# A two-layer graph network: the second layer's first product made of seven products of quarters, x read twice, the column factors stored with the adjacency

## The chip, the cores and the metric

The kernel runs on one core of a Trainium2 chip. The time is device microseconds of that core. TensorE (PE) multiplies; VectorE (DVE), ScalarE (ACT) and GpSimd (POOL) do the elementwise work; SyncE (SP) issues most loads, and POOL issues the stores. Each engine works through its own list of instructions in order and waits on semaphores for the others. All data is float32.

## What is computed

The input is x, 16 graphs of 1024 nodes with 256 channels, and one adjacency matrix of 1024 by 1024.

```
# layer 0
h = max(layernorm(x), 0)
c = mean of h over channels
A_s = weights made of sigmoid(c[m] - c[n]);  g = relu((h.T @ (adj * A_s)) * para)
q = g.T;  k, v = h @ kv_w;  4 heads of 64
x = x + softmax(q k.T * scale) v
# layer 1
h = max(layernorm(x), 0)
A_hat = (adj + I) * dinv[:, None] * dinv[None, :]       # dinv from row and column sums
agg = A_hat @ h
y1 = agg @ W1.T + b1                                    # 256 -> 512 channels
y2 = relu(batchnorm(y1)) @ W2.T + b2                    # statistics over all graphs
x = x + batchnorm(y2)
```

## The kernel before

**Stages.** A short beginning handles graph 0's first norm, keys and queries. Then `attention` (L1092) goes through 16 graphs of 16 steps. A step computes scores of two blocks of 128 keys (`scores`, L923, PE L933, exponentials on ACT L941), adds up the exponentials on DVE (`Unit.add`, L962 and L965) and multiplies the exponentials of the step before with the values (`Unit.values`, PE L976). Between these, each step takes pieces from a generator, `background(b)` (L835), which holds everything else that must happen while graph b's attention runs. A `total` of costs (1.71 for two products of 128x128 by 512) is spread over the 16 steps: each step takes pieces until its share is done. After the last graph, `second` (L1221) does the second batch-normalised product and the output.

**What the background of graph b holds, in this order.** Keys and values of graph b+1 (`keys_values`, L649), its queries (`queries`, L514: the product with the weighted adjacency, as seven products of quarters), the second norm of graph b-1 (`normed`, L790), the aggregation of graph b-1 (`aggregate`, L682: again seven products of quarters, with the combined quarters of A_hat read from `aht_d` in DRAM), the first norm of graph b+2 (`summed`) and, in `prepare` (L812), the first product of layer 1 for graph b-1 (`hidden`, L757) woven with the first weights of graph b+2 (`weigh`, L454: ACT L485 and L493, then DVE L472).

**`hidden` before.** For each half of the nodes and each of four blocks of 128 output channels, two products of 128x128 by 512 are accumulated in one PSUM bank, evicted with the bias by ACT (L773), stored by a POOL DMA (L774), and read by DVE for the batch statistics (L777): 16 products and 8 evictions for a graph. All background products take turns in three PSUM banks (`ps_mm`, `bank`, L164), so a product waits until the one three before it has been evicted.

**The graph's matrix.** In graph 0's background, `degrees` (L225) sums rows and columns and forms dinv; `graph` (L244) reads the adjacency in 8 pieces, adds the identity, forms the seven combined quarters with four subtractions on POOL (L278, L279, L282, L283) and stores them to `aht_d` (L285 to L287). The two run side by side with graph 1's queries. The row factor dinv[n] goes into the second norm's scale (`shift`, L325, DVE L328). The column factor is applied to the aggregate after the products: `scale` (L705) multiplies the four quarters of `at` with `dbc`, dinv broadcast to all partitions, which `load_later` (L290) fetches through DRAM (`dinv_d`).

**x.** `load_x` (L173) loads a graph's x once into a pool of three buffers; it serves the first norm, receives the attention's output (`add_output`, L1058) and then feeds the second norm. `keep` (L786) stores it to DRAM.

Of the kernel before, what the change touches and what calls it, by code (L numbers as in the profile page):

```python
# [10 lines left out]
F32 = mybir.dt.float32  # L11
# [6 lines left out]
P = 128  # L18
# [5 lines left out]
def gnn_two_layers_kernel(  # L24
# [72 lines left out]
    def layers(shifted):  # L97
# [20 lines left out]
        ps_mm = st.enter_context(tc.tile_pool(name=f"ps_mm_{kind}", bufs=3, space=PSUM))  # L118

        xs, hs, hts, ats, qs, ks, vs = {}, {}, {}, {}, {}, {}, {}  # L120
        invs = {}
        csums, cbcs, weighted, weighers = {}, {}, {}, {}
        s1s = {}
# [48 lines left out]

        def load_x(b):  # L173
            xs[b] = p3.tile([P, NT, C], F32, tag="x", name=f"x_{b}")
            parts = 4 if b == 0 else 2
            for part in range(parts):
                t = slice(part * NT // parts, (part + 1) * NT // parts)
                nc.sync.dma_start(
                    out=xs[b][:, t], in_=x[b].rearrange("(t p) c -> p t c", p=P)[:, t]
                )  # L180
# [44 lines left out]
        def degrees():  # L225

            nc.vector.tensor_reduce(row, rows.rearrange("p q t -> p t q"), AX.X, ALU.add)
            ahead = [load_adj_t(t, "at") for t in range(2)]
            yield 0.0
            for t in range(NT):  # L230
                a = ahead[t]
                blk = a[:, t * P : (t + 1) * P]
                nc.scalar.activation(a, a, AF.Copy, accum_out=col[:, t : t + 1])
                db = p1.tile([P, P], F32, tag="s1", name=f"db_{t}")
                nc.vector.tensor_mul(db, blk, ident)
                nc.vector.tensor_reduce(diag[:, t : t + 1], db, AX.X, ALU.add)
# [4 lines left out]
            nc.vector.tensor_sub(deg, deg, diag)  # L241
            rsqrt(dinv, deg, 1.0, tmp_deg)

        def graph():  # L244
# [21 lines left out]
            for u in range(2 * HT):  # L266
# [21 lines left out]
                yield 0.0  # L288

        def load_later():  # L290
            later["w1"] = big.tile([P, CC, H1], F32, tag="w1", name="w1")
            nc.sync.dma_start(out=later["w1"], in_=w1_t.rearrange("(k p) j -> p k j", p=P))
            later["dbc"] = const.tile([P, N], F32, tag="dbc", name=f"dbc_{kind}")
            nc.sync.dma_start(out=dinv_d.rearrange("(t p) -> p t", p=P), in_=dinv)
            nc.sync.dma_start(
                out=later["dbc"], in_=dinv_d.rearrange("(o n) -> o n", o=1).to_broadcast([P, N])
            )

        class Norm:
# [3 lines left out]
            def __init__(self, b, first):  # L303
                tag = "a" if first else "b"
                self.src = xs[b]
                self.st6 = p1.tile([P, NT, 6], F32, tag="st6", name=f"st6_{tag}_{b}")
# [375 lines left out]
        def aggregate(b):  # L682


            pieces = []
            order = (0, 2, 5, 1, 4, 6, 3)

# [24 lines left out]
            def second(m):  # L712
                add(c11, m, c12)
                sub(a12, a12, a11)
                soon(lambda: scale(c11, 0))

            def fifth(m):
                add(c22, m, c21)
                add(c12, m, c12)
                soon(lambda: scale(c22, 1))  # L720

            def sixth(m):
                add(c21, m, c21)
                soon(lambda: scale(c21, 0))

            def seventh(m):
                add(c12, m, c12)
                scale(c12, 1)

            for i, (left, after) in enumerate(  # L730
# [12 lines left out]
                for th in range(NP // 2):  # L743
# [68 lines left out]
        def prepare(b, products):  # L812
# [3 lines left out]
            yield from islice(products, 1)  # L816
            if b == 2:
                for k in range(CC):
                    yield from weave(islice(products, 3), (0, islice(w, AHEAD // 2)))
                    yield TOP  # L820
                    transposed(b, (k,))
                    yield 1.0
                yield from products
                return
            squares(b)
            yield from weave(islice(products, 3), (0, islice(w, AHEAD // 2)))
            gathered(b, 0)
            yield from weave(islice(products, 1), (0, islice(w, 1)))
            gathered(b, 1)
            yield from weave(islice(products, 2), (0, islice(w, AHEAD // 2 - 1)))  # L830
            yield from products
# [3 lines left out]
        def background(b):  # L835

            if b == 0:
                differences(1)
                for k in range(CC):
# [15 lines left out]
            gather = aggregate(b - 1)  # L855
            if b + 1 < B:
                w, products, norm = weighers[b + 1], keys_values(b + 1), normed(b - 1)
                yield from weave(islice(products, 4), (0, islice(w, 4)))
                if b == 1:
                    load_later()  # L860
                yield from weave(queries(b + 1), (0, double(w)), (9, islice(norm, 5)))
                yield next(gather)
                yield from weave(products, (0, norm))
            else:
                yield from weave(endings.pop(), (2, normed(b - 1)))
                yield next(gather)
            if b + 2 < B:
# [224 lines left out]
        def attention():  # L1092
# [7 lines left out]
            for s in range(len(steps) + 2):  # L1100
                if s < len(steps):
                    unit, g = steps[s]
                    b = unit.at[0]
                    if s % per_graph == 0:
# [25 lines left out]
                if before is not None:  # L1130
                    (last, g_last), prs = before
                    last.values(g_last, prs)
                    if g_last == NG - 1:
# [29 lines left out]
        with st:  # L1163
# [22 lines left out]
            else:  # L1186
# [23 lines left out]
                run(weave(products, (0, islice(weighers[0], AHEAD))))  # L1210
                load_x(1)
                load_x(2)
                run(weave(plain_queries(0), (0, weighers[0]), (5, Norm(1, True).all())))
                attention()
                attn.close()
# [348 lines left out]
```

## Time and profile before

| what | value |
|---|---|
| median of 3 runs | 2489.24 us (2488.99 to 2489.55) |
| the profiled execution | 2488.76 us |
| its span, first to last instruction | 2487.0 us |
| mean granted TensorE clock | 0.993 |
| PE busy, share of the span | 2435.7 us, 98% |
| DVE, ACT, POOL busy | 1882.0, 1401.7, 429.2 us |
| moved by DMA | 421.42 MB, 169 GB/s on average |

A group in the profile names a line, an engine, an operation, the tiles out<-in, how often it occurred, the busy time, the mean duration of one in ns, and the idle time of the engine just before, with what ended it. In the timeline the columns are the start and the duration in us. A float32 product appears as two matmul records for each half of 64 columns, four for a product of 128x128 by 512. In a table of stretches, each engine's busy time is given with the number of its instructions in brackets.

### The profile page before, as it was taken

To read this page: it belongs to the slowest core of one execution; us is meant where nothing else is said; L and a number is where in the kernel's file an instruction comes from. 1 tells how busy PE (TensorE), PEld (TensorE's weight loads), DVE (VectorE), ACT (ScalarE), POOL (GpSimd) and SP (SyncE) were. 2 spreads that over 40 slices of the span, in tenths; PEclk is the share of its full clock that TensorE was granted. 3 is DMA by queue.
4 is the path that set the end of the run, shared out by engine and by line. 5 is a ranking of instruction groups with operands and counts; after the bars stand their busy time and mean duration, and the time that the engine had idled before them with its cause. 6 is when DMAs were issued, how large, how long until landed. Compare 5 with 4: busy or idle time off the path is not lost. (4 is left out here: it accounts for less than half of the span.)

```text
span 2487.0 us, 35569 instructions
## 1 busy us (share of the span) xinstructions
PE 2435.7 (98%) x13403; PEld 841.2 (34%) x13403; DVE 1882.0 (76%) x2920; ACT 1401.7 (56%) x1927; POOL 429.2 (17%) x527
## 2 busy tenths in 40 slices
PE   9999999999999999999999999999999999999995
PEld 4333333333333333333333333333333332334444
DVE  5668787877778787878787787868787877767775
ACT  7775564647473746656474747465564634345544
POOL 1640101010101001011101010110101001036652
PEclk9999999999999999999999999999999999999997
DMA  4754535354545545362645445543536344355559
GB/s 150 238 173 172 170 114 199 101 199 129 197 145 178 164 159 169 116 206 84 215 126 182 145 174 169 178 153 132 191 94 210 116 140 162 132 214 220 189 199 374
DMA packets 187909, 421.42 MB, mean 169 GB/s; under 512 B 21832, under 2 KB 81744, under 8 KB 181968
## 3 DMA queue, kind: packets, MB, share of 16 engines
q1 hardware_dynamic: 158560, 311.56, 37.9%
q0 software_dynamic: 29168, 107.50, 11.6%
q8 instruction: 108, 1.77, 0.3%
q14 instruction: 73, 0.60, 0.1%
HBM read 315.63 MB, written 103.35 MB: 168 GB/s over the span
## 5 line engine op out<-in xcount | busy, mean ns | idle before, releaser
L941 ACT ACTIVATE p<-sc 128x1024 f32<-128x1024 f32 x512 | 494.9, 1019 | 617.6 <-PE sc L933 617.2
L965 DVE TENSOR_TENSOR acc<-acc,p 128x1024 f32<-128x1024 f32 x384 | 471.3, 1227 | 165.1 <-ACT p L941 143.8
L933 PE MATMUL sc<-q,k 64*64 64x512 f32 x4096 | 498.8, 602 | 6.2 <-ACT p L941 6.2
L976 PE MATMUL o<-p,v 128*64 128x512 f32 x2048 | 494.5, 604 | 0.3 <-DVE os L990 0.3
L171 PE MATMUL pg<-w,h_a 128*64 128x512 f32 x1600 | 359.8, 592 | 0.8 <-DVE w L472 0.8
L171 PE MATMUL pa<-aht,h_b 128*64 128x512 f32 x1536 | 346.0, 592 | 1.1 <-ACT h_b L342 1.0
L485 ACT ACTIVATE w<-cbc,csum 128x512 f32<-128x512 f32 x256 | 285.8, 1168 | 0.0
L933 PEld LDWEIGHTS sc<-q,k 64*64 64x64 f32 x4096 | 131.0, 132 | 347.9 <-issue 286.5
L472 DVE SCALAR_TENSOR_TENSOR w<-w,adj 128x1024 f32<-128x1024 f32 x128 | 156.9, 1225 | 95.0 <-ACT w L493 91.1
L171 PE MATMUL py<-at,w 128*64 128x512 f32 x1024 | 228.4, 592 | 0.2 <-ACT y L773 0.2
L976 PEld LDWEIGHTS o<-p,v 128*64 128x64 f32 x2048 | 124.4, 136 | 298.3 <-issue 260.3
L994 POOL DMA_DIRECT2D out_d<-os x58 | 34.2, 590 | 1070.8 <-DVE os L990 1037.5
L171 PEld LDWEIGHTS pg<-w,h_a 128*64 128x64 f32 x1600 | 114.8, 137 | 229.2 <-issue 218.8
L171 PEld LDWEIGHTS pa<-aht,h_b 128*64 128x64 f32 x1536 | 109.9, 137 | 215.3 <-issue 202.0
L773 ACT ACTIVATE y<-py,vec 128x512 f32<-128x512 f32 x128 | 87.4, 683 | 115.4 <-PE py L171 91.8
L493 ACT ACTIVATE w<-w 128x1024 f32<-128x1024 f32 x128 | 135.1, 1055 | 1.7
L774 POOL DMA_DIRECT2D y_d<-y x128 | 69.7, 545 | 371.8 <-ACT y L773 362.6
L548 DVE TENSOR_TENSOR w<-w,w 128x1024 f32<-128x1024 f32 x112 | 132.7, 1214 | 1.5
L171 PEld LDWEIGHTS py<-at,w 128*64 128x64 f32 x1024 | 74.0, 137 | 145.5 <-issue 131.5
L171 PE MATMUL pv<-kvw_f,ht 128*64 128x256 f32 x1024 | 116.1, 379 | 0.0
L171 PE MATMUL pk<-ht,kvw_f 128*64 128x512 f32 x512 | 115.2, 592 | 0.2 <-ACT ht L404 0.2
L342 ACT ACTIVATE h_b<-x,lnsm_b 128x256 f32<-128x256 f32 x128 | 69.9, 599 | 65.9 <-DVE lnsm_b L331 65.9
(169 smaller groups left out, 2665.4 us busy)
## 6 DMA issues: line engine op xcount, KB each, us to landing
aht<-aht_d SPq DMA_DIRECT2D x224, 512.0 KB, 6.4
adj<-in_adj_dram SPq DMA_DIRECT2D x128, 512.0 KB, 4.8
y_d<-y POOLq DMA_DIRECT2D x128, 256.0 KB, 3.0
yin_f<-y_d SPq DMA_DIRECT2D x32, 1024.0 KB, 6.4
para<-in_para_dram SPq DMA_DIRECT2D x64, 256.0 KB, 3.6
x_d<-x POOLq DMA_DIRECT2D x16, 1024.0 KB, 5.2
xo_f<-x_d SPq DMA_DIRECT2D x32, 512.0 KB, 8.2
out_dram<-xo_f POOLq DMA_DIRECT2D x32, 512.0 KB, 10.8
```

The source lines that it names most:

```text
L171: nc.tensor.matmul(dst[r], left[:, r], right, start=start, stop=stop)
L342: nc.scalar.activation(self.h[:, t, :], self.src[:, t, :], AF.Relu, bias=self.sm[:, 1, t : t + 1], scale=self.sm[:, 0, t : t + 1], accum_o ...
L472: nc.vector.scalar_tensor_tensor(w, w, 1.0, a, op0=ALU.add, op1=ALU.mult)
L485: nc.scalar.activation(w[:, t, :].rearrange("p (t q) -> p t q", q=P), cbc[:, q * NT // NH : (q + 1) * NT // NH], AF.Abs, bias=csum[:, th * ...
L493: nc.scalar.activation(made[i], made[i], AF.Tanh, scale=-0.5 / C)
L548: nc.vector.tensor_sub(block(i)[part], block(x)[part], block(y)[part])
L773: nc.scalar.activation(y, made, AF.Identity, bias=b1[:, j : j + 1])
L774: nc.gpsimd.dma_start(out=y1_d[i][:, j, :], in_=y)
L933: nc.tensor.matmul(sc[part, e, :], ks[b][k][r, m * P + c * HW : m * P + (c + 1) * HW], qs[b][k][r, f * FB : (f + 1) * FB], start=True, sto ...
L941: nc.scalar.activation(pr, sc, AF.Exp)
L965: nc.vector.tensor_add(self.acc, self.acc, pr)
L976: nc.tensor.matmul(self.o[r, :], vs[b][k][:, m, r], pr[:, e, :], start=(m == 0), stop=(m == NT - 1),)
```

## The change

In `hidden`, graphs 0 to 13 now compute the first product of layer 1 from quarters of W1 and of the aggregate: seven products for each of two blocks of 128 columns, 14 in all, none accumulated with another. Four combinations of W1's quarters are formed once on POOL (`load_later`); four combinations of the aggregate's quarters are formed on DVE for each graph (`steps_of` and the first line of `hidden`). Two of the seven products are evicted by ACT, five by DVE, which adds the parts that belong together; POOL adds two further pairs for each block. Graphs 14 and 15 keep the old form (`plain_hidden`).

The column factor moves from `aggregate` into `graph`: each piece of the adjacency is multiplied by `dbc` on POOL (two multiplications a piece) before it is combined, so `graph` now has to follow `degrees` and the fetching of `dbc`, and runs from the end of graph 0's background into graph 1's. The first norm and the first weights of graph 2 get other places in graph 0's background, and graph 2's transposition is no longer a special case of `prepare`. The order of the last two products of `aggregate` is swapped.

x is loaded twice: once for the first norm (`xn`) and once for the attention's output and the second norm (`xr`), with one buffer each instead of three common ones. The buffers `y` grow from four to six. The first unit of a graph adds its output to x one step later (`wait` 6 instead of 5).

```
...
-    vec = const.tile([P, 18], F32, name="vec")
-    nc.sync.dma_start(out=vec, in_=vecs)
+    vec = const.tile([P, 20], F32, name="vec")
+    nc.sync.dma_start(out=vec[:, :18], in_=vecs)
...
+    b1_step = vec[:, 18:20]
+    nc.gpsimd.tensor_sub(b1_step, b1[:, HC // 2 :], b1[:, : HC // 2])
...
-        py = st.enter_context(tc.tile_pool(name=f"py_{kind}", bufs=4))
+        py = st.enter_context(tc.tile_pool(name=f"py_{kind}", bufs=6))
...
-        def load_x(b):
-            xs[b] = p3.tile([P, NT, C], F32, tag="x", name=f"x_{b}")
+        def load_x(b, first=False):
+
+            into, tag = (firsts, "xn") if first else (xs, "xr")
+            into[b] = p1.tile([P, NT, C], F32, tag=tag, name=f"{tag}_{b}")
...
             rsqrt(dinv, deg, 1.0, tmp_deg)
+            dbc = big.tile([P, 4, H1 // 2], F32, tag="w1s", name="dbc")
+            dbc = later["dbc"] = dbc.rearrange("p a b -> p (a b)")
+            nc.sync.dma_start(out=dinv_d.rearrange("(t p) -> p t", p=P), in_=dinv)
+            nc.sync.dma_start(
+                out=dbc, in_=dinv_d.rearrange("(o n) -> o n", o=1).to_broadcast([P, N])
+            )
...
+                dinvs = later["dbc"].rearrange("p (m c) -> p m c", m=NH)[:, :, cols]
+                for n in range(2):
+                    nc.gpsimd.tensor_mul(a[:, n], a[:, n], dinvs)
+                yield 0.0
...
+        def w1_quarters():
+
+            HH = H1 // 2
+            return [later["w1"][:, k, m * HH : (m + 1) * HH] for m in (0, 1) for k in (0, 1)]
+
         def load_later():
             later["w1"] = big.tile([P, CC, H1], F32, tag="w1", name="w1")
             nc.sync.dma_start(out=later["w1"], in_=w1_t.rearrange("(k p) j -> p k j", p=P))
-            later["dbc"] = const.tile([P, N], F32, tag="dbc", name=f"dbc_{kind}")
-            nc.sync.dma_start(out=dinv_d.rearrange("(t p) -> p t", p=P), in_=dinv)
-            nc.sync.dma_start(
-                out=later["dbc"], in_=dinv_d.rearrange("(o n) -> o n", o=1).to_broadcast([P, N])
-            )
+            later["s"] = big.tile([P, 4, H1 // 2], F32, tag="w1s", name="w1s")
+            s1, s2, s3, s4 = (later["s"][:, i] for i in range(4))
+            a11, a12, a21, a22 = w1_quarters()
+            nc.gpsimd.tensor_add(s1, a21, a22)
+            nc.gpsimd.tensor_sub(s2, s1, a11)
+            nc.gpsimd.tensor_sub(s3, a11, a21)
+            nc.gpsimd.tensor_sub(s4, a12, s2)
...
-            order = (0, 2, 5, 1, 4, 6, 3)
+            order = (0, 2, 5, 1, 4, 3, 6)
...
-            def scale(c, g):
-                nc.vector.tensor_mul(c, c, later["dbc"][:, g * FB : (g + 1) * FB])
...
+                    (a12, seventh),
                     (a22, sixth),
-                    (a12, seventh),
...
+                    elif i == 6 and b < B - 2:
+                        steps_of(b)
                     yield 1.71
 
+        def steps_of(b):
+
+            b11, b12, _, b22 = at_quarters(b)
+            t1 = p1.tile([P, NT // 2, P], F32, tag="s1", name=f"at1_{b}")
+            t1 = t1.rearrange("p t c -> p (t c)")
+            t2 = p2.tile([P, FB], F32, tag="para", name=f"at2_{b}")
+            nc.vector.tensor_sub(t1, b12, b11)
+            nc.vector.tensor_sub(t2, b22, t1)
+            nc.vector.tensor_sub(b12, b22, b12)
+            steps[b] = t1, t2
...
         def hidden(b):
+
+            if b >= B - 2:
+                yield from plain_hidden(b)
+                return
...
+            b11, t3, b21, b22 = at_quarters(b)
+            t1, t2 = steps[b]
+            t4 = p2.tile([P, FB], F32, tag="para", name=f"at4_{b}")
+            nc.vector.tensor_sub(t4, b21, t2)
...
+            def put(y, n, j):
+                i = b * NH + n
+                nc.gpsimd.dma_start(out=y1_d[i][:, j, :], in_=y)
+                soon(lambda: nc.vector.bn_stats(stats1[:, j, i, :], y))
+
+            add = nc.vector.tensor_add
+
+            def m1(c):
+                part = one("1", a11, c, b11)
+                nc.scalar.activation(
+                    new("11", c), part, AF.Identity, bias=b1[:, c : c + 1]
+                )
+
+            def m2(c):
+                y = made["11"]
+                add(y, one("2", a12, c, b21), y)
+                put(y, 0, c)
+
+            def m3(c):
+                y = made["12"]
+                add(y, one("3", s4, c, b22), y)
+                put(y, 1, c)
+
+            def m4(c):
+                y = made["21"]
+                add(y, one("4", a22, c, t4), made["sum"])
+                put(y, 0, 2 + c)
+
+            def m5(c):
+                nc.scalar.copy(new("22", c), one("5", s1, c, t1))
+                if c == 1:
+                    both(c)
+
+            def both(c):
+                nc.gpsimd.tensor_add(new("12", c), made["21"], made["22"])
+
+            def m6(c):
+                y = new("21", c)
+                add(y, one("6", s2, c, t2), made["11"])
+                if c == 0:
+                    both(c)
+
+            def m7(c):
+                part, y = one("7", s3, c, t3), made["22"]
+                nc.vector.scalar_tensor_tensor(
+                    new("sum", c), part, b1_step[:, c : c + 1], made["21"], op0=ALU.add, op1=ALU.add
+                )
+                nc.gpsimd.tensor_add(y, y, made["sum"])
+                put(y, 1, 2 + c)
+
+            for c, order in ((0, (m1, m5, m6, m2, m3, m7, m4)), (1, (m1, m6, m2, m5, m7, m3, m4))):
+                for each in order:
+                    each(c)
+                    yield 0.86
...
             yield from Norm(b, False).all()
-            if b + 3 < B:
-                load_x(b + 3)
+            load_x(b + 1)
...
             squares(b)
-            yield from weave(islice(products, 3), (0, islice(w, AHEAD // 2)))
+            yield from weave(islice(products, 5), (0, islice(w, AHEAD // 2)))
...
-                yield from weave(
-                    islice(products, 4), (0, double(islice(w, 8))), (0, islice(norm, 4))
-                )
-                yield from weave(
-                    plain_queries(1), (0, norm), (0, w), (5, graph()), (7, degrees())
-                )
+                yield from weave(islice(products, 4), (0, double(islice(w, 8))))
+                yield from weave(plain_queries(1), (0, w), (4, norm), (7, degrees()))
                 differences(2)
-                yield from islice(products, 2)
-                yield from prepare(2, products)
+                w, build = weighers[2], graph()
+                later["graph"] = build
+                yield from weave(islice(products, 1), (0, islice(build, 1)))
+                yield from weave(islice(products, 2), (0, islice(w, 2)), (0, islice(build, 2)))
...
+            if b + 2 < B:
+                load_x(b + 2, True)
...
-                yield from weave(islice(products, 4), (0, islice(w, 4)))
+                build = later.pop("graph", iter(()))
+                yield from weave(islice(products, 4), (0, islice(w, 4)), (0, islice(build, 4)))
+                yield from weave(
+                    queries(b + 1), (0, double(w)), (0, build), (9, islice(norm, 5))
+                )
                 if b == 1:
                     load_later()
-                yield from weave(queries(b + 1), (0, double(w)), (9, islice(norm, 5)))
...
-                        total += 13.7 * (0 < b < B - 2) + 27.4 * (b == B - 1) + 3.0 * (b == 0)
+                        total += 12.0 * (0 < b < B - 2) + 25.7 * (b == B - 1) + 3.0 * (b == 0)
...
-                            wait = 5 if last.by_squares and last.at[1:] == (0, 0) else 4
-                            at_mid.setdefault(s + wait - 1, []).append(last.sums)
+                            opens = last.by_squares and last.at[1:] == (0, 0)
+                            wait = 6 if opens else 4
+                            at_mid.setdefault(s + 3 + opens, []).append(last.sums)
...
```

More of the change, by code (lines that the diff above doesn't have):

```diff
@@ L118, in layers @@
         ps_mm = st.enter_context(tc.tile_pool(name=f"ps_mm_{kind}", bufs=3, space=PSUM))
+        firsts = {}
         xs, hs, hts, ats, qs, ks, vs = {}, {}, {}, {}, {}, {}, {}
         invs = {}
-        csums, cbcs, weighted, weighers = {}, {}, {}, {}
+        csums, cbcs, weighted, weighers, steps = {}, {}, {}, {}, {}
         s1s = {}
@@ L178, in load_x @@
                 nc.sync.dma_start(
-                    out=xs[b][:, t], in_=x[b].rearrange("(t p) c -> p t c", p=P)[:, t]
+                    out=into[b][:, t], in_=x[b].rearrange("(t p) c -> p t c", p=P)[:, t]
                 )
@@ L304, in __init__ @@
                 tag = "a" if first else "b"
-                self.src = xs[b]
+                self.src = firsts[b] if first and b in firsts else xs[b]
                 self.st6 = p1.tile([P, NT, 6], F32, tag="st6", name=f"st6_{tag}_{b}")
@@ L714, in second @@
                 sub(a12, a12, a11)
-                soon(lambda: scale(c11, 0))
             def fifth(m):
@@ L719, in fifth @@
                 add(c12, m, c12)
-                soon(lambda: scale(c22, 1))
             def sixth(m):
                 add(c21, m, c21)
-                soon(lambda: scale(c21, 0))
             def seventh(m):
                 add(c12, m, c12)
-                scale(c12, 1)
             for i, (left, after) in enumerate(
@@ new lines, in at_quarters, with left, one, new @@
+        def at_quarters(b):
+            return [ats[b][n][:, k] for k in (0, 1) for n in (0, 1)]
+        def hidden(b):
+            if b >= B - 2:
+                yield from plain_hidden(b)
+                return
+            HH = H1 // 2
+            a11, a12, _, a22 = w1_quarters()
+            s1, s2, s3, s4 = (later["s"][:, i] for i in range(4))
+            b11, t3, b21, b22 = at_quarters(b)
+            t1, t2 = steps[b]
+            t4 = p2.tile([P, FB], F32, tag="para", name=f"at4_{b}")
+            nc.vector.tensor_sub(t4, b21, t2)
+            def left(block, c):
+                return block[:, c * P : (c + 1) * P]
+            def one(name, block, c, right):
+                part = bank(f"py_{b}_{c}_{name}")
+                product(part, left(block, c), right, True, True)
+                return part
+            made = {}
+            def new(name, c):
+                made[name] = py.tile([P, FB], F32, tag="y", name=f"y_{b}_{c}_{name}")
+                return made[name]
+            def put(y, n, j):
[42 more added lines that the diff above has]
+                    yield 0.86
@@ L759, in hidden, with plain_hidden @@
+        def plain_hidden(b):
             at = ats[b]
@@ L816, in prepare @@
             yield from islice(products, 1)
-            if b == 2:
-                for k in range(CC):
-                    yield from weave(islice(products, 3), (0, islice(w, AHEAD // 2)))
[L820 to L824, printed above, removed]
+            yield from islice(products, 1)
             squares(b)
-            yield from weave(islice(products, 3), (0, islice(w, AHEAD // 2)))
+            yield from weave(islice(products, 5), (0, islice(w, AHEAD // 2)))
             gathered(b, 0)
-            yield from weave(islice(products, 1), (0, islice(w, 1)))
+            yield from weave(islice(products, 3), (0, islice(w, 1)))
             gathered(b, 1)
-            yield from weave(islice(products, 2), (0, islice(w, AHEAD // 2 - 1)))
+            yield from weave(islice(products, 3), (0, islice(w, AHEAD // 2 - 1)))
             yield from products
@@ L843, in background @@
                 w, products, norm = weighers[1], keys_values(1), Norm(2, True).all()
-                yield from weave(
-                    islice(products, 4), (0, double(islice(w, 8))), (0, islice(norm, 4))
-                )
-                yield from weave(
-                    plain_queries(1), (0, norm), (0, w), (5, graph()), (7, degrees())
-                )
-                differences(2)
-                yield from islice(products, 2)
-                yield from prepare(2, products)
+                yield from weave(islice(products, 4), (0, double(islice(w, 8))))
+                yield from weave(plain_queries(1), (0, w), (4, norm), (7, degrees()))
+                differences(2)
+                w, build = weighers[2], graph()
+                later["graph"] = build
+                yield from weave(islice(products, 1), (0, islice(build, 1)))
+                yield from weave(islice(products, 2), (0, islice(w, 2)), (0, islice(build, 2)))
+                yield TOP
+                transposed(2, (0,))
+                yield 1.0
+                yield from weave(islice(products, 1), (0, islice(w, 1)), (0, islice(build, 1)))
+                yield from islice(w, 1)
+                yield TOP
+                transposed(2, (1,))
+                yield 1.0
+                yield from islice(w, AHEAD - 4)
+                yield from products
                 return
+            if b + 2 < B:
+                load_x(b + 2, True)
             before = hidden(b - 1)
@@ L864, in background @@
             else:
+                yield next(gather)
                 yield from weave(endings.pop(), (2, normed(b - 1)))
-                yield next(gather)
             if b + 2 < B:
@@ L1210, in layers @@
                 run(weave(products, (0, islice(weighers[0], AHEAD))))
-                load_x(1)
-                load_x(2)
+                load_x(1, True)
                 run(weave(plain_queries(0), (0, weighers[0]), (5, Norm(1, True).all())))
+                load_x(2, True)
                 attention()
```

## The prediction

> **What bounds the kernel now.** I read the engine totals, then the groups, then a table of stretches, then two pieces of the timeline.
>
> ```profile
> PE 2435.7 (98%) x13403; PEld 841.2 (34%) x13403; DVE 1882.0 (76%) x2920; ACT 1401.7 (56%) x1927; POOL 429.2 (17%) x527
> L171 PE MATMUL py<-at,w 128*64 128x512 f32 x1024 | 228.4, 592 | 0.2 <-ACT y L773 0.2
> ```
>
> TensorE is never idle, so time falls with PE work, as long as the others keep up. `hidden` has 1024 records in 256 products: 0.89 us each. Within the run of 24 records at 962.47 they follow every 0.86 us (six products in 5.32 us, the last overlapping), which I take.
>
> ```profile
> 951.65:958.83 7.18, 7.18 (x43) 2.15 (x41) 4.41 (x6) 1.94 (x2) 0.63 (x1) 1.00 0.66 211
> 958.83:967.72 8.89, 8.89 (x50) 2.72 (x49) 8.61 (x11) 4.23 (x5) 1.52 (x3) 1.00 0.41 121
> 967.72:976.62 8.90, 8.90 (x51) 2.73 (x49) 5.97 (x7) 8.00 (x10) 1.18 (x3) 1.00 0.88 269
> 976.62:983.91 7.29, 7.29 (x46) 2.25 (x45) 4.64 (x7) 7.29 (x9) 1.63 (x3) 1.00 0.86 287
> 848.00:984.00 136.00, 136.00 (x790) 44.01 (x792) 107.24 (x168) 78.36 (x107) 14.16 (x22) 1.00 0.50 159
> ```
>
> The first four stretches are the last four steps of a graph's attention (12 to 15); the last is a whole graph's length. After the length come PE, PEld, DVE, ACT and POOL. The clock is full. DVE has room over a graph (107 of 136 us), but in step 13 it is busy 8.61 of 8.89 us.
>
> ```profile
> 964.08 2.37 DVE L412 STREAM_TRANSPOSE sq<-h_a 128x1024 f32<-128x1024 f32 x2
> 966.71 2.34 ACT L485 ACTIVATE w<-cbc,csum 128x512 f32<-128x512 f32 x2
> 967.72 1.95 PE L933 MATMUL sc<-q,k 64*64 64x512 f32 x16
> 969.52 1.05 ACT L493 ACTIVATE w<-w 128x1024 f32<-128x1024 f32 x1
> 970.47 1.93 ACT L941 ACTIVATE p<-sc 128x1024 f32<-128x1024 f32 x2
> 971.52 2.56 DVE L965 TENSOR_TENSOR acc<-acc,p 128x1024 f32<-128x1024 f32 x2 [2.58 <-ACT p L941]
> 974.00 1.22 DVE L472 SCALAR_TENSOR_TENSOR w<-w,adj 128x1024 f32<-128x1024 f32 x1
> ```
>
> Here the weights hold up ACT, so step 14's exponentials start 2.75 us after its scores, and DVE's additions end 6.4 us after them. Now that harms nobody: `hidden` is evicted by ACT.
>
> ```profile
> 139.73 0.17 DVE L241 TENSOR_TENSOR deg<-deg 128x8 f32<-128x8 f32 x1
> 174.42 0.41 SPq L294 DMA_DIRECT2D dinv_d<-deg  x1
> 185.48 0.34 SPq L295 DMA_DIRECT2D dbc_f<-dinv_d  x1
> 222.22 1.04 POOL L95 TENSOR_TENSOR lnsm_b<-lnsm_b,neg_half 128x4 f32<-128x4 f32 x1
> 224.31 0.13 DVE L328 TENSOR_TENSOR lnsm_b<-lnsm_b,deg 128x4 f32<-128x4 f32 x1
> 230.41 0.69 DVE L582 TENSOR_TENSOR q<-pg,q 128x512 f32<-128x512 f32 x1
> ```
>
> At the start the degrees are known at 140, and 4 KB of dinv take 11.0 us to land. POOL is free when the second norm of graph 0 asks it for a root at 222, and DVE goes on at 224.
>
> **Part 1, the products.** 14 graphs lose 2 of 16 products: 28 x 0.86 = 23.9 us off PE, all on the path.
>
> **Part 2, evictions beside them.** Per graph DVE loses four scalings (674 ns) and gains four combinations and ten evictions (692 ns; with a scalar 751): +6.9 us, 114 of 134: fits on average, so it matters where. ACT loses four of eight evictions (683): free. POOL gains four additions of 512 columns; between 0.73 us (256 columns) and 2.36 (1024) I estimate 1.27; it works 14 us a graph, so this is hidden unless DVE waits for the sum. The number and size of y stores stay.
>
> Now steps 13 and 14, with 0 at step 13's scores, in the new order of instructions. PE: scores 1.9, values 1.8, the aggregate's last unit 1.71, to 5.4; products 1, 5, 6, 2 to 8.8; step 14's scores and values to 12.55; products 3, 7, 4 to 15.1; then 1 and 6 of the second block, each needing the bank of the product three before: 3's and 7's. ACT: evictions of 1 and 5 to 7.9, weights 2.34 and 1.05 to 11.2, exponentials to 12.1 and 13.1. DVE: last quarter 6.3, combination 6.95, squares 2.37 to 9.3, evictions of 6 and 2 to 10.6, fold 1.4 to 12.0, step 14's two additions 2.56 from 12.2 to 14.7, eviction of 3 at 15.3, weight 1.22 to 16.5, statistics 0.62, eviction of 7 at 17.85. So PE, ready for the second block's 6 at 15.96, waits until about 17.95: 2.0 us. Behind it stand step 15's scores. In step 15 each bank is free in time by the same reckoning, and DVE's lag ends in the next step, where it waits for ACT's tanh (ready 10 us into the step). Bounds: 1.2 (if DVE's 512-column pieces follow each other every 0.62 us throughout, as three at 221.66 do) and 2.8 (if a POOL addition meets one of DVE's additions; alone 1219 ns, beside POOL up to 2410 ns). This repeats in 13 graphs (1 to 13 of the attention); `hidden(13)` runs beside graph 15 without weights and keeps its gain. 13 x 2.0 = 26 us (16 to 36).
>
> The Trainium skill (SBUF — State Buffer, section "SBUF: two separate sides") says the port pair that DVE and GpSimd share is locked for a whole instruction when DVE has two SBUF inputs. By it, a graph in which one POOL addition meets the chain would wait an estimated 1.27 more, 16.5 us over 13 graphs; I count none, as by the times above POOL's first addition (10.1 to 11.4) runs beside evictions from PSUM.
>
> **Part 3, the start.** POOL's chain for 8 pieces lasted from 84.66 to 155.49, 70.8 us, back to back. It gains 16 multiplications of 512 columns (20.3 us), loses the first load and identity (5, done while waiting) and about 4 of waits for its own stores: 82. It can begin to multiply when `dbc` has landed: degrees 139.9, root 1.9, dinv 1.4 (the 4 KB of csum) to 11.0 (itself, beside a 512 KB load), I take 6, the broadcast 5.8 (the like of cbc): 154 (149 to 159). End 236, store of x issued and root 2.5: 239. Graph 0's second norm stands behind it in POOL's queue, and DVE's L328, so far at 224, waits from 223.3: 15.7 us. Behind L328 on DVE stand a step's additions and the last query eviction (L582, 230.4), whose bank PE wants at 234: 3 us of slack. That is 13 us lost (2 to 25: 77 us of chain without any port collision; 91 with more of them). Behind dinv and `dbc` on SP's queue also wait csum and cbc of graph 2: cbc lands at about 159 instead of 136, ACT's first weight stands for it from 146 with step 13's exponentials behind, and PE is some 10 us late (1 to 16) by then. This shifts what follows, so the two are not added: together 13. The low end goes to -3, since the new places of graph 2's norm and weights may remove the two waits of PE for ACT before graph 1 (2.5 us at 159.8, 2.1 at 166.9).
>
> What moves with `graph`: its 16 loads and 24 stores on POOL's queue (0.73 and 0.58 to 0.78 us each, in the 70.8) now stand ahead of graph 1's first output store, the store of x, the two roots and the four combinations of W1 (0.73 each, behind W1's own load, landing in 11.3 us). The output store, at 212 so far, comes up to 25 us later; SP waits for it before it loads W1 and the first pieces for the aggregate, which need the last store landed (5.0 us) and 6.4 us more: 236 + 11 = 247, against the aggregate's start at 241.5 plus the 13 lost. It is just covered; where the 13 shrinks, this takes its place.
>
> The Trainium skill (DMA: Bandwidth & Descriptors, section "Latency and other measured facts") puts a transfer's fixed cost at about 2 us. By it dinv lands 4 us earlier than I take and the start costs an estimated 9; the row's 11.0 would make it 18.
>
> **Part 4, the second reading of x.** 15 MB more at 159 GB/s average is under 7 us of a graph's 136 on queues half idle. SP issues `xr` after the norm's last pieces, about step 8; 512 KB land in 5.6 us; `add_output` needs it in step 10, some 10 us later. `xn` goes ahead of adjacency loads whose weights come a step later. Cost 0; without cover DVE stands for each late us. Removing the scalings and swapping the last aggregate products: 0, beside PE; after graph 15, where nothing covers it, up to 1.
>
> **Sum** on the profiled execution, 2488.8 (span 2487.0 and 1.8 around it): -23.9 + 26 + 13 = 2503.9. The median shown is 0.5 above: 2504.4.
>
> **Rivals.** (a) Faster: the bank wait in step 14 does not arise, only the start does: 2489.2 - 23.9 + 13 = 2478. It turns on when DVE evicts product 7; with the start at 13, below (23.9 - 13) / 13 = 0.8 us a graph the change gains. For it: now no step has such a wait, though DVE runs up to 11 us behind in the queries. Against: there a product lasts 3.4 us and a bank has 6.8 to spare; here 0.86 and 1.7. (b) The start is hidden and the bank wait stays: 2489.2 - 23.9 + 26 + 2 = 2493. (c) Neither: 2489.2 - 23.9 + 2 = 2467. (d) `xr` comes after step 10's `add_output`: from 10 us late on it counts, 14 times; at 2 us, +28: 2532. Against it the 10 us.
>
> **How the numbers follow.** Forecast 0.53, (a) 0.16, (b) 0.12, (c) 0.13, (d) 0.06. The forecast's own range: 2489.2 - 23.9 + 16 - 3 = 2478 to 2489.2 - 23.9 + 36 + 25 = 2526. The range given, 2470 to 2525, takes in (a) and (b) and leaves out (c) and (d). A measurement here tells 0.2% (5 us) from no change. Faster: (c), nearly all of (a): 0.28; same: (b), part of the forecast's low end: 0.12; slower: 0.60.
>
> **What would show it.** PE matmuls of `py` down by 112 records; in each of 13 graphs one wait of PE for DVE of about 2 us within `py`; in the first 260 us POOL's multiplications from about 154, L328's successor waiting for POOL some 10 to 16 us, ACT waiting for cbc. I am wrong if a graph's length in the middle is 134.3 us instead of about 136.3, or if graph 2 of the attention starts before 306.

## The result, and the profile after

The changed kernel takes **2522.04 us** (2521.06 to 2522.87) against 2489.22 us before (2488.99 to 2489.55): a ratio of **1.0132, interval 1.0114 to 1.0149**. It is 32.8 us slower. The forecast was 2504 (2470 to 2525): the right side, but less than half of the loss.

The totals on the page of the changed kernel, and its group of the new products:

```profile
PE 2424.2 (96%) x13291; PEld 831.9 (33%) x13291; DVE 1989.0 (79%) x3052; ACT 1371.0 (54%) x1871; POOL 527.5 (21%) x604
L174 PE MATMUL py<-at,w1s 128*64 128x512 f32 x448 | 106.6, 595 | 17.0 <-DVE y_sum L860 17.0
```

112 records of PE are gone, as wanted, and 17.0 us of PE's idle time stand ahead of the new products, waiting for DVE: 13 times 1.3 us. But PE's share fell from 98% to 96%, and these 17 us are only a part of it. Where the rest is, a table of stretches tells (length, then busy time of PE, PEld, DVE, ACT and POOL with the number of instructions, then the granted clock, DMA share and GB/s). The changed kernel:

```profile
140.00:160.00 20.00, 8.11 (x62) 3.33 (x58) 2.94 (x4) 1.49 (x4) 5.51 (x8) 0.77 0.40 100
160.00:190.00 30.00, 24.40 (x152) 8.73 (x152) 23.38 (x16) 25.51 (x33) 29.28 (x34) 0.87 0.72 243
...
200.00:215.00 15.00, 10.43 (x58) 2.98 (x54) 14.72 (x10) 10.32 (x10) 14.85 (x15) 1.00 0.60 209
215.00:230.00 15.00, 7.85 (x24) 1.91 (x28) 14.93 (x10) 0.28 (x1) 14.81 (x18) 0.54 0.40 132
...
482.00:618.00 136.00, 134.59 (x778) 43.24 (x776) 113.53 (x176) 76.17 (x105) 19.09 (x26) 1.00 0.49 166
```

The kernel before, in the same stretches:

```profile
140.00:160.00 20.00, 17.54 (x132) 7.53 (x128) 9.33 (x11) 13.57 (x20) 15.88 (x20) 1.00 0.57 186
160.00:190.00 30.00, 27.92 (x166) 9.04 (x164) 21.23 (x24) 27.90 (x33) 0.00 (x0) 1.00 0.29 78
...
200.00:215.00 15.00, 15.00 (x86) 4.71 (x84) 14.79 (x23) 4.50 (x5) 1.56 (x2) 1.00 0.17 57
215.00:230.00 15.00, 15.00 (x100) 5.82 (x100) 14.69 (x33) 6.44 (x12) 3.17 (x4) 1.00 0.32 88
```

Three things are to be seen. In a steady graph PE is idle for 1.4 us of 136. Between 140 and 160 PE is busy for 8.1 us only: it stands still from 148.1 to 164.5, and DVE with it. And from 200 to 230 PE is idle or slow while DVE is busy all the time, with 10 instructions in 15 us where it had 23 and 33: DVE's instructions have become long. In both places the granted clock falls as well.

Graph 2's first scores begin at 304.11 us before and at 336.60 after: **32.5 us are lost ahead of it**, and from there to the end only 0.2 more (span 2487.0 to 2519.7). The distances between the first scores of successive steps, each against the same step before, divide the 32.5: 12.0 us up to graph 1's step 1 (A), 15.9 in the next four steps, which take 50.4 instead of 34.6 (B), 4.5 in step 7, which takes 13.4 instead of 8.9 (C), and 0.1 in the rest of graph 1. A is a net figure: before the stall the changed kernel was 2.8 us ahead. PE's side of it, in the timeline of the changed kernel (start, duration, tiles, number of records, idle time before and what ended it):

```profile
164.51 3.63 PE L1052 MATMUL sc<-q,k 64*64 64x512 f32 x16 [16.40 <-ACT p L1060]
...
217.77 3.68 PE L174 MATMUL pg<-w,s_a 128*64 128x512 f32 x8 [4.48 <-DVE w L570]
225.83 3.68 PE L174 MATMUL pg<-w,h_a 128*64 128x512 f32 x8 [4.38 <-DVE h_a L580]
...
263.11 5.36 PE L174 MATMUL pv<-kvw_f,ht 128*64 128x256 f32 x32 [2.55 <-DVE q L604]
```

**A** is the wait for graph 2's column means that the prediction describes: behind dinv and `dbc` on SP's queue.

```profile
138.50 0.38 SPq L250 DMA_DIRECT2D dinv_d<-deg  x1
150.33 0.33 SPq L251 DMA_DIRECT2D dbc<-dinv_d  x1
150.71 0.42 SPq L471 DMA_DIRECT2D csum_d<-csum  x1
155.47 0.32 SPq L472 DMA_DIRECT2D cbc<-csum_d  x1
...
159.75 2.32 ACT L507 ACTIVATE w<-cbc,csum 128x512 f32<-128x512 f32 x2 [16.41 <-DMA cbc<-csum_d]
```

dinv needs 11.8 us to land, and cbc, which goes at 127 when nothing stands ahead of it (run 1), is asked for at 155.47. ACT stands for it for 16.4 us, with the exponentials behind.

**B** the prediction does not have. DVE's instructions in the timeline of the changed kernel, and one of POOL's that ran beside them:

```profile
186.60 3.38 DVE L1190 TENSOR_TENSOR xr<-os,xr 128x512 f32<-128x512 f32 x1
...
210.28 5.78 DVE L1084 TENSOR_TENSOR acc<-acc,p 128x1024 f32<-128x1024 f32 x2
...
221.10 3.45 DVE L579 TENSOR_TENSOR h_a<-s_a,h_a 128x512 f32<-128x512 f32 x1
221.51 2.48 POOL L287 TENSOR_TENSOR au_f<-au_f,dbc 128x512 f32<-128x512 f32 x2
...
256.23 0.16 DVE L350 TENSOR_TENSOR lnsm_b<-lnsm_b,deg 128x4 f32<-128x4 f32 x1 [1.45 <-POOL lnsm_b L97]
```

The same three operations before:

```profile
170.28 0.69 DVE L1071 TENSOR_TENSOR x<-os,x 128x512 f32<-128x512 f32 x1
...
192.18 2.56 DVE L965 TENSOR_TENSOR acc<-acc,p 128x1024 f32<-128x1024 f32 x2 [2.27 <-ACT p L941]
...
197.53 0.68 DVE L557 TENSOR_TENSOR h_a<-s_a,h_a 128x512 f32<-128x512 f32 x1
```

Set against the median of the same line and shape over the whole trace, 29 of DVE's 90 instructions from 155 to 262 are more than 0.2 us too long, by 29.6 us together. All of them read two tiles in SBUF and ran while POOL computed on its pieces; the other 61 are no longer than usual. From 231.2 to 240.3 POOL computes nothing, since it stands for the output, and there DVE's instructions of the same kind take their usual time again (`xr<-os,xr` at 237.34: 0.69). In the kernel before no instruction of DVE from 155 to 262 is too long, and POOL's pieces had been finished at 155; but 12 of 68 from 80 to 155 were, by 5.4 us, nearly all beside the same pieces without multiplications. That view was to be had before the prediction.

**C** is the last line of DVE's in the changed kernel: its wait for POOL's root, 1.45 us, and PE's wait at 263.11 for the query eviction behind it. It is where the prediction had put its 13 us.

The steady part is as described. Step 14 of a graph in the changed kernel:

```profile
1002.71 2.55 DVE L1084 TENSOR_TENSOR acc<-acc,p 128x1024 f32<-128x1024 f32 x2 [0.19 <-ACT p L1060]
1005.18 0.68 DVE L836 TENSOR_TENSOR y<-py,y 128x512 f32<-128x512 f32 x1
1005.78 1.21 DVE L494 SCALAR_TENSOR_TENSOR w<-w,adj 128x1024 f32<-128x1024 f32 x1
1006.92 0.68 DVE L819 BATCH_NORM_STATS2 stats<-y 128x6 f32<-128x512 f32 x1
1007.52 0.73 DVE L860 SCALAR_TENSOR_TENSOR y_sum<-py,vec,y 128x512 f32<-128x512 f32 x1
...
1008.31 1.08 PE L174 MATMUL py<-at,w1s 128*64 128x512 f32 x4 [1.31 <-DVE y_sum L860]
```

The exponentials' additions, the third product's eviction, a weight, the statistics, then the seventh product's eviction, and PE's second product 6 after it. At 0.86 us a product PE could have started at 1006.5, so the wait costs 1.8 us (the 1.31 leave out the tail of the last record). The graph's length is 136.1 us.

### The profile page after: what moved, and what is told of

Its sections match the earlier page's. It is cut to its first block, busy times and chain, and to the rows that moved or that the text cites. A ratio compares the mean times of both kernels' runs of the same rounds, so it can differ in the third digit from the quotient of the medians.

```text
span 2519.7 us, 35730 instructions
## 1 busy us (share of the span) xinstructions
PE 2424.2 (96%) x13291; PEld 831.9 (33%) x13291; DVE 1989.0 (79%) x3052; ACT 1371.0 (54%) x1871; POOL 527.5 (21%) x604
## 5 line engine op out<-in xcount | busy, mean ns | idle before, releaser
L1084 DVE TENSOR_TENSOR acc<-acc,p 128x1024 f32<-128x1024 f32 x384 | 477.1, 1242 | 122.2 <-ACT p L1060 100.7
L507 ACT ACTIVATE w<-cbc,csum 128x512 f32<-128x512 f32 x256 | 287.0, 1174 | 16.4 <-DMA cbc<-csum_d 16.4
L1113 POOL DMA_DIRECT2D out_d<-os x58 | 34.1, 588 | 930.8 <-DVE os L1109 901.3
L494 DVE SCALAR_TENSOR_TENSOR w<-w,adj 128x1024 f32<-128x1024 f32 x128 | 164.5, 1285 | 41.4 <-ACT w L515 40.6
L174 PE MATMUL py<-at,w1s 128*64 128x512 f32 x448 | 106.6, 595 | 17.0 <-DVE y_sum L860 17.0
L174 PE MATMUL py<-at,w 128*64 128x512 f32 x464 | 115.3, 595 | 1.8 <-DVE y L836 0.5
L1081 DVE TENSOR_TENSOR acc<-p,p 128x1024 f32<-128x1024 f32 x64 | 78.6, 1228 | 40.2 <-ACT p L1060 40.2
L364 ACT ACTIVATE h_a<-xn,lnsm_a 128x256 f32<-128x256 f32 x120 | 70.6, 594 | 66.8 <-DVE lnsm_a L353 66.8
L1424 ACT ACTIVATE yin_f<-yin_f,sm_f 128x512 f32<-128x512 f32 x128 | 93.4, 803 | 18.9 <-DMA yin_f<-y_d 18.8
```

The lines of the kernel that those rows point to most:

```text
L174: nc.tensor.matmul(dst[r], left[:, r], right, start=start, stop=stop)
L494: nc.vector.scalar_tensor_tensor(w, w, 1.0, a, op0=ALU.add, op1=ALU.mult)
L507: nc.scalar.activation(w[:, t, :].rearrange("p (t q) -> p t q", q=P), cbc[:, q * NT // NH : (q + 1) * NT // NH], AF.Abs, bias=csum[:, th * ...
L1081: nc.vector.tensor_add(self.acc, self.held, pr)
L1084: nc.vector.tensor_add(self.acc, self.acc, pr)
L1424: nc.scalar.activation(y, y, AF.Relu, bias=sh[:, j : j + 1], scale=scale[:, j : j + 1])
```

## The experiments

Each run is compared with runs of the kernel before on the same chip. What the start loses is read from graph 2's first scores against 304.1. Line numbers differ by a few between the runs' kernels. A line of waits gives who waits for whom, then the us in total, how often, and the longest.

**1. The column means ahead of dinv.** The fetching of dinv and `dbc` is taken out of `degrees` and called after `differences(2)`.

```
             rsqrt(dinv, deg, 1.0, tmp_deg)
+        def fetch():
             dbc = big.tile([P, 4, H1 // 2], F32, tag="w1s", name="dbc")
...
                 differences(2)
+                fetch()
                 w, build = weighers[2], graph()
```

> Changed kernel, with graph 2's column means (csum, cbc) sent on SP's queue ahead of dinv and dbc instead of behind them. Theory: the start lost about 34 us in three places: A, 13 us at 146 to 165, where ACT waits 16.4 us for cbc; B, about 16.5 us at 200 to 230, where DVE is slowed by POOL's multiplications; C, 4.5 us at 256 to 268, where DVE waits for POOL's root. If the three simply add, A goes and the time is 2509. If POOL's chain, which still begins when dbc lands at 155, is the real limit, C grows by what A loses and the time is about 2520. I expect the second: cbc lands at about 136, no ACT wait for it, and a longer wait of DVE for POOL's root, 2515 to 2522. Rival (the late cbc alone is the loss, with B its aftermath, a burst of postponed weights): 2489 to 2495.

2516.67 us, ratio 1.0106 (1.0090 to 1.0123); graph 2 begins at 332.25, so the start still loses 28.1. SP's queue and the waits in this run:

```profile
123.28 0.42 SPq L474 DMA_DIRECT2D csum_d<-csum  x1
126.77 0.33 SPq L475 DMA_DIRECT2D cbc<-csum_d  x1
138.48 0.37 SPq L253 DMA_DIRECT2D dinv_d<-deg  x1
```

```profile
PE pv L174 <- DVE q L607: 15.0, 1, 15.0
...
DVE lnsm_b L353 <- POOL lnsm_b L97: 13.8, 1, 13.8
```

A is gone: graph 1's step 1 comes 19.3 us earlier than in the changed kernel, 7.3 ahead of the kernel before. Steps 3 to 6 then lose 15.5 us against the kernel before and step 7 loses 18.1: DVE's wait for POOL's root has grown from 1.4 to 13.8 us, with PE behind it for 15.0. So removing the stall brings 5 us: POOL's chain, which starts when `dbc` lands, is the limit behind it. The rival, that the late means are the whole loss, falls.

**2. No multiplications** on POOL; the result then lacks the column factor.

```
-                dinvs = later["dbc"].rearrange("p (m c) -> p m c", m=NH)[:, :, cols]
-                for n in range(2):
-                    nc.gpsimd.tensor_mul(a[:, n], a[:, n], dinvs)
                 yield 0.0
```

> Changed kernel without POOL's 16 multiplications by dbc; the pieces are still built behind dbc's landing, and the column factor is left out of the result. Theory: B is DVE waiting for POOL's port during the multiplications, C the end of POOL's longer chain: both go, A stays, 2522 - 16 - 5 = 2501 (2496 to 2506). DVE's additions of two SBUF tiles in 165 to 235 take 1.2 us again instead of 1.7 to 4.6. Rival (B is the aftermath of A and not of the multiplications): only C goes, 2517.

2505.33 us, ratio 1.0065 (1.0048 to 1.0082); graph 2 begins at 320.35, a loss of 16.2. The first wait is all that remains of the large ones:

```profile
PE sc L1049 <- ACT p L1057: 17.0, 1, 17.0
PE pg L174 <- DVE w L567: 2.0, 1, 2.0
```

DVE's excess from 155 to 262 falls from 29.6 to 7.3 us, the loss in steps 1 to 4 from 15.9 to 3.7, and step 7 loses nothing. The multiplications are thus worth 16.3 us of the 32.5, most of B and all of C, though POOL is off the path by itself until C. The pieces no longer read `dbc` either, so they do not stand behind its landing as the expectation has it: their first subtraction comes at 153.3, where the first multiplication came at 155.4.

**3. Both.**

> Both edits together: column means of graph 2 first, and no multiplications by dbc (column factor left out of the result). Theory: A, B and C all go, what remains is the products' gain and the bank wait, 2489 - 24 + 24 = 2489 (2486 to 2496). Rival (the start's loss has another cause, for instance that the pieces are built later at all, beside graph 2's weights): above 2500.

2496.76 us, ratio 1.0031 (1.0019 to 1.0042), slightly over the range I gave; graph 2 begins at 310.81. So 6.7 us remain at the start that neither edit takes away. DVE's excess is still 13.2 us in this run: the pieces' additions and subtractions on POOL, which now run beside graph 2's weights, hold DVE up as well. That these make up the 6.7 is argued, not tested by itself.

The four runs make a table of the start's loss (us, graph 2's first scores less 304.1):

| | multiplications | none |
|---|---|---|
| column means behind dinv | 32.5 | 16.2 |
| column means ahead | 28.1 | 6.7 |

The late means cost 4.4 or 9.5, the multiplications 16.3 or 21.4, depending on the other: each hides a part of the other.

**4. The start of before, the seven products kept.** `graph` and `degrees` run beside graph 1's queries again, `load_later` fetches `dbc`, and `aggregate` multiplies the quarters by it on DVE.

```
+            def scale(c, g):
+                nc.vector.tensor_mul(c, c, later["dbc"][:, g * FB : (g + 1) * FB])
...
             def sixth(m):
                 add(c21, m, c21)
+                scale(c21, 0)
...
             def seventh(m):
                 add(c12, m, c12)
+                scale(c12, 1)
```

> The seven products with the start of before: the pieces are built beside graph 1's queries, dinv and dbc are fetched afterwards, and the column factor is applied to the aggregate by DVE again (four multiplications of 512 columns a graph, two of them right before the combinations). x is read twice, as in the changed kernel. Theory: no loss at the start, and the bank wait of 1.8 us becomes 1.8 to 3.2 with up to 1.4 us more on DVE ahead of it: 2489 - 24 + 24 to 42, 2489 to 2507, I take 2497. Rival (the loss lies in the steady part after all): 2515 and more.

2495.53 us, ratio 1.0026 (1.0016 to 1.0035). Graph 2 begins at 303.80: the start loses nothing. A graph takes 136.5 us instead of 136.1: with the scalings back on DVE, PE waits in 13 graphs for product 3's eviction too, 0.6 us each time, besides the 1.3 for product 7's. The loss of the changed kernel is in the start; the seven products with the old start lose 6.3 us.

**5. The weights two products later**, on the changed kernel:

```
-            yield from weave(islice(products, 5), (0, islice(w, AHEAD // 2)))
+            yield from weave(islice(products, 5), (2, islice(w, AHEAD // 2)))
```

> Changed kernel; of the weights woven between the seven products, the first three slots come two products later, so ACT makes no weights ahead of step 14's exponentials and DVE evicts product 7 before it multiplies a weight. Theory: DVE reaches product 7's eviction some 2 us earlier, PE's wait of 1.8 us in step 14 of 13 graphs goes, the start stays as it is: 2522 - 23.6 = 2498.5 (2496 to 2504), a graph 134.3 us. Rival (the postponed weights make a new wait of the same size one step on): 2515 to 2522.

2509.27 us, ratio 1.0080 (1.0063 to 1.0097): 12.8 us faster than the changed kernel, half of what I expected. A graph takes 135.3 us, not 134.3. Part of the difference is at the start, which loses 29.6 here. The waits of the whole run:

```profile
PE py L174 <- DVE y L831: 5.2, 13, 0.4
...
PE py L174 <- DVE y_sum L860: 2.2, 13, 0.2
```

The wait for product 7 is nearly gone (0.2 us each), and a smaller one stands in step 15, for product 2 of the second block. The cause was named rightly, its removal was overrated. What is left fits a DVE that is behind by its amount of work, which runs 9 and 10 try.

**6. The old products in the changed kernel** (`plain_hidden` for all graphs). Three of the four combinations (`steps_of`) are still formed, and one of them overwrites a quarter which the old form then reads; the work is that of the old form and these three.

> Changed kernel with the old form of the first product (16 products, eight evictions by ACT) in all graphs; start, column factors, x read twice as changed. Theory: products +24, bank wait -23.6, start the same: 2522, within 5. Steady graph 136.0. Rival (the second reading of x or the removed scalings move the steady graph): a graph's length other than 136.0, 0.5 us a graph would be 7.

2528.55 us, ratio 1.0156 (1.0139 to 1.0173): 6.5 us slower than the changed kernel, more than the 5 I allowed. A graph takes 136.6 us, 0.6 above before. Which of the combinations and the second reading of x makes these 0.6, this run does not tell; it bounds both from above. The start loses 31.4, as with the seven products.

**7 and 8. The old start with the later weights**, by two products and by one.

> The start of before and the column factor on the aggregate (as in the run with the old start), with the weights two products later. Theory: start loss 0, wait 2.2 us a graph gone but for what the two scalings ahead of product 7 leave: 2495.5 - 13 x 2.2 = 2467 (2465 to 2478), faster than both kernels. Rival (a new wait on DVE or ACT takes the place): 2485 to 2495.

> The same with the weights one product later instead of two. DVE's weight then still stands behind product 7's eviction, but ACT's first weight is made ahead of step 14's exponentials. Theory: the wait shrinks by the weight's 1.2 us and not wholly: 2495.5 - 13 x 1.2 = 2480. Rival (ACT's late exponentials don't matter): like the run with two, 2467.

2488.31 us, ratio 0.9997 (0.9987 to 1.0006), and 2486.99, ratio 0.9991 (0.9981 to 1.0001); a graph takes 136.0 and 135.9. Here the rival of the first holds: of 2.2 us a graph only 0.5 go. The second missed its 2480 as well. In the run by two PE now waits 0.6 us for product 3's eviction, 0.2 for product 7's and 0.4 for product 2's in step 15, and DVE, from the last quarter of the aggregate on (819.36 in the run by two), has no pause until the end of these. Not the place of one weight seems to be the limit but the sum of DVE's work in two steps.

**9 and 10. Combinations on POOL**, on run 8: all four, or the two that products 7 and 4 want (below).

```
-            nc.vector.tensor_sub(b12, b22, b12)
+            nc.gpsimd.tensor_sub(b12, b22, b12)
...
-            nc.vector.tensor_sub(t4, b21, t2)
+            nc.gpsimd.tensor_sub(t4, b21, t2)
```

> The run with the old start and the weights one product later, and the four combinations of the aggregate's quarters on POOL instead of DVE. What remained there is a DVE that works without a pause from the last quarter of the aggregate to product 7's eviction; PE waits 1.3 us in step 14 and 0.5 in step 15 of 13 graphs. Theory (DVE's amount of work in this stretch is the limit): 2.7 us less on DVE, the waits go, 2487 - 13 x 1.7 = 2465 (2462 to 2472). Rival (POOL's reading of SBUF holds up DVE's additions of two SBUF tiles, as at the start): DVE's additions of exponentials in this step take up to 2.4 us instead of 1.27 and little or nothing is gained, 2480 to 2490.

> The same with only the two combinations on POOL that are wanted late (for products 7 and 4). Theory: 1.35 us less on DVE, the wait in step 14 shrinks from 1.3 to about 0, half of the rest in step 15 stays: 2487 - 13 x 1.3 = 2470 (2466 to 2477). Rival (port): 2480 to 2490.

With four: 2481.02 us, ratio 0.9968 (0.9956 to 0.9981). With two: **2477.94 us, ratio 0.9956 (0.9939 to 0.9972)**, faster than both kernels. So the work on DVE was a limit, but taking more off it gave less. The run with four shows why, DVE first, then POOL:

```profile
820.76 3.68 DVE L1082 TENSOR_TENSOR acc<-acc,p 128x1024 f32<-128x1024 f32 x2 [1.05 <-ACT p L1058]
...
821.10 2.25 POOL L784 TENSOR_TENSOR at<-at 128x512 f32<-128x512 f32 x1
```

The run with two:

```profile
820.93 2.55 DVE L1082 TENSOR_TENSOR acc<-acc,p 128x1024 f32<-128x1024 f32 x2
...
834.76 1.08 PE L174 MATMUL py<-at,w1s 128*64 128x512 f32 x4 [0.17 <-DVE y_sum L862]
```

With four combinations, POOL's second and third fall onto DVE's additions of exponentials, which take 3.68 instead of 2.55 us, and POOL's own subtraction 2.25 instead of 1.27; with two, the additions come alone. It is so in every graph from 2 to 13, and step 14 takes 8.7 us with four and 8.5 with two. The forecasts of 2465 and 2470 were too low by 16 and 8: a graph takes 135.4 and 135.2, and the waits for products 2 and 7 remain (0.3 and 0.2 us).

## Why the prediction was wrong

**Part 1, the products: right.** 112 records less; a graph of 136.1 with a wait of 1.8 makes 134.3, against 136.0 before: 1.7 us, twice 0.86. No run shows a graph of 134.3 itself; the shortest in the steady part is 135.2.

**Part 2, the bank wait: right.** One wait a graph, for the seventh eviction, in 13 graphs, of 1.8 us where I had 2.0 (1.2 to 2.8); the eviction ended 17.7 us after the beginning of step 13's scores (990.54), where I had 17.85. 13 x 1.8 = 23 took back the products' 24. Run 5 shows that it is the weight and the exponentials ahead of it; runs 5, 7 and 8 show that DVE has little more room behind, which the prediction did not ask. Its +6.9 us of DVE's work a graph adds up to 7.1 from its own terms; the stretches have 6.3, 113.5 against 107.2.

**Part 3, the start: the step that failed.** The term was 13 us and measured 32.5. Its beginning was right: `dbc` landed at 155.4 (predicted 154), ACT waited for cbc, and POOL's pieces came late. But the path that was to cost the 13 hardly waited: L328's successor (L350), put at 15.7 us behind POOL's root, waited 1.45, since DVE had itself become late by then. The loss lies ahead of it, in A (12.0, put at 10) and in B (15.9, put at nothing). Of the two sentences that made the price, the first is the step that failed.

- "It gains 16 multiplications of 512 columns (20.3 us)" priced POOL's chain and nothing else. A multiplication lasts 1.24 us alone (estimated: 1.27), but the pieces took from 155.4 to 253.9, 98 us instead of 82, even over the 91 that I had allowed "with more of them"; 9.2 of it is POOL's wait for the output (L1113) that DVE made late. Above all, the collisions were counted on POOL's side alone. DVE lost 29.6 us to them, at a time when PE depends on DVE for the queries. Part 2 had the price, "alone 1219 ns, beside POOL up to 2410 ns", and used it for step 14 only. Run 2 puts what the multiplications cost at 16.3.
- "so the two are not added: together 13", in the prediction's words. Run 1 shows how this stands: when the late means are mended, the wait for the root is 13.8 and takes most of their place, as I had argued. So the sentence was nearly right (a stall that costs 12.0 net is worth 4.4), but what remains is a loss of 28, not of 13.

The port rule that I weighed, the Trainium skill's SBUF — State Buffer, section "SBUF: two separate sides", says that the loser of the port pair waits for the other's whole instruction. I asked it about the steady graph, where I counted none, and there the additions do keep their 2.55 us. I did not ask it what DVE loses at the start, where it speaks against the change. The trace agrees with it there and goes further: 3.45 us for 0.68 is a delay of 2.8, a little longer than the two multiplications that ran meanwhile (2.48 together), though by the records DVE had begun 0.4 us before the first of them.

**Output store and W1: covered**, as said. POOL issued the output at 240.3, W1 was asked for at 260.6 and PE took the first aggregate at 272.2 without a wait for it.

**Part 4, x: right as far as seen.** Nothing waits for the loading of `xr` but graph 0's first norm, for 4.0 us at the very start (4.2 before). Run 6 leaves at most 0.6 us a graph for it, if nothing else in the steady graph gained.

**The rivals.** (a), (b) and (c) needed a hidden start or no bank wait; run 4 is (b) nearly made real, at 2495.5 against the 2493 worked out. (d) did not arise.

## What to carry to other kernels

When work is put on one engine, price also what it costs the engines beside it (here POOL's 98 us cost DVE 29.6): look in the trace for instructions that are longer than their own median, and ask who ran beside them. A stall that is removed uncovers the next one behind it, so find the second limit before counting the gain (a stall that cost 12.0 was worth 4.4 here, and 1.8 a graph was worth 0.8). Seven products instead of eight turn PE's time into evictions and combinations; whether that pays is decided by the room that DVE has in those steps, and here, with the old start, it paid only once combinations had left DVE, most where POOL did not meet DVE's additions.

## What the runs showed of the hardware

After some waits PE itself was slow for a while. The 16 records of scores after the wait of 16.40 us took 3.63 us instead of 1.95; the 8 records after the waits of 4.48 and 4.38 took 3.68 instead of 1.89; 32 records of 256 columns after the wait of 2.55 took 5.36 instead of 3.62. After a wait of 2.86 us (at 207.49) nothing was lost. The granted clock of 215 to 230 was 0.54. That is 1.7 to 1.8 us for each of four waits, 7.0 of the 32.5 us, which the prediction had not counted with its stalls. The Trainium skill's TensorE: Matmul & The Clock Gate, section "Part 1: The HAM clock gate (the "warmup" mystery)", says that the clock is halved after an idle window of about 3.4 us and comes back after a busy one; a window at half the clock loses half of it, an estimated 1.7 us, and that agrees with these rows. The wait of 2.55 us that was enough is shorter than it says.

In this trace the clock is half from 150.89 to 167.96, from 215.74 to 229.40 and from 263.53 to 266.94: five, four and one times 3.41 us, and all of these moments lie on one grid of 3.41. The stretch of the grid tells the waits of 2.86 and 2.55 apart:

```profile
205.50:208.90 3.40, 1.41 (x8) 0.57 (x8) 3.29 (x3) 2.91 (x3) 3.40 (x4) 1.00 0.78 238
260.10:263.50 3.40, 0.85 (x10) 0.32 (x6) 3.26 (x6) 3.24 (x7) 0.00 (x0) 1.00 0.66 182
263.50:266.90 3.40, 3.40 (x20) 1.96 (x18) 2.78 (x3) 1.92 (x5) 1.22 (x1) 0.50 1.05 418
```

The longer wait, from 204.63 to 207.49, is cut by the grid at 205.5, and PE was busy for 1.41 us of the stretch that holds most of it; the shorter lies within one stretch, with PE busy for 0.85. Two waits do not settle a rule.

A store of dinv, 4 KB as 1024 single elements, landed 11.8 us after its issue in the changed kernel and 10.1 in run 1, where the same 4 KB of csum, eight elements a row, took 3.5 at the start and 1.4 in the median of its 14 stores.
